# Two colours for tokens in the expert stage of a fused convolution-attention and mixture-of-experts kernel

## The chip, the core and the metric

The kernel runs on one core of one Trainium2 chip. The metric is the device time of one execution in microseconds (us); three runs of the kernel before gave 1347.75, 1349.04 and 1352.04 us, median 1349.04 us. PE is TensorE's matmul, PEld its weight load, DVE is VectorE, ACT ScalarE, POOL GpSimd, SP SyncE.

## What is computed

The input is x, 4 images of 256 channels and 64 x 64 pixels, float32. Layer 0 normalises x, then each pixel attends to its 3 x 3 neighbours, and the result is added to x. Layer 1 takes the 16384 pixels as tokens of width 256: a gated sum over a window of 64 tokens is added, and then a mixture of 8 experts of which each token uses two:

```
logits = tokens @ router_w.T;  rw, re = top_k(softmax(logits), 2)
rw = rw / rw.sum(-1)
out = tokens
for e in range(8):
    h = gelu(tokens @ w1[e] + b1[e])
    y = h @ w2[e] + b2[e]
    out = out + combine[:, e:e + 1] * y        # combine: rw at the two chosen experts, else 0
```

So every token's row of the output is the sum of its own row and of two experts' rows.

## The kernel before

The tokens are worked on in NB = 32 blocks of 512 (NT = 4 tiles of 128). A loop over g (L1064) weaves four generators, each a step at a time: `attend(g)` (the attention), `ranks(g - 2)`, `tail(g - 1)` (window sum, second normalisation, router, the store of the token's own row by L699) and `produce(g + 1)` (projections). A fifth stream, `experts` (L903), is let run by `follow` up to a number of steps that is due at this point of the loop; the knots of that plan follow from `GROUPS`. The framework then fixes the order of instructions on each engine; an engine takes its instructions in that order and waits on semaphores.

Experts work on **slots** of UP = 256 rows of one expert, in two halves of 128 (U = 2). The way there: `tail` ends with `hot` (which expert is a token's first and second choice) and `chosen` (their sum, L737). `ranks` counts on PE, with a triangle of ones and a square of ones (L764, L767), how many tokens before this one chose each expert, adds up the tiles of the block on DVE (`so_far`, L773), and so has the row of each token in its expert's region of `rows_in`, a buffer in HBM (L776 to L782). `give` (L796) scatters 128 tokens with their weights and their row number to these rows by one indirect DMA of GpSimd; a block needs 8. Rows of blocks 0 to 3 go out at once, `paced` behind a recent ACT instruction; those of later blocks are put on the list `waiting`, from which `give_rows` takes two behind every slot's adds (L1022), or all that a fetch needs (L923).

Blocks come in groups (GROUPS, L85: 13 groups of two blocks and 6 of one). When a group's blocks are ranked, L833 to L877 work out on one partition how many slots each expert has full, and write for each slot the expert and the first row to a table. Group k has 2 n 512/256 slots for its n blocks; the first has 7 fewer and the last 14 more, since only full slots are run before the last group. For the last group, `blank` rows are stored behind each expert's rows by SP (L826, eight DMAs of 256 rows), so that part-filled slots read rows of weight zero whose row number lies behind the output. There are 135 slots, 18 of them in the last group.

A slot runs so: SP reads expert and row from the table and fetches the slot's 2 x 128 rows (L926, one of 7 buffers; it waits for the scattered rows of its group); PE transposes them (L950), ACT copies; PE multiplies with w1 (L962), ACT applies gelu (L968); PE multiplies with w2 (L981); DVE adds the bias (L985) and scales by the token's weight (L986), for each half; GpSimd adds each half's 128 rows to the output by an indirect DMA with add (L999). These three PE steps belong to three slots in one round: transposes of slot m + 2, first product of m + 1, second of m.

[...]`add` therefore puts a wait into both adds of a slot, on both adds of the slot before:

```python
behind = adds[-U:]
...
for t in range(U):
    inst = nc.gpsimd.indirect_dma_start(out=out, ..., compute_op=ALU.add).ins
```

Within a slot all tokens are different, so its two halves need not wait for each other.

Of the kernel before, what the change touches and what calls it, by code (L numbers as in the profile page):

```python
# [44 lines left out]
FP = mybir.dt.float32  # L47
AF = mybir.ActivationFunctionType
ALU = mybir.AluOpType
# [3 lines left out]
P = 128  # L53
# [9 lines left out]
def hybrid_block_kernel(ctx: ExitStack, tc: tile.TileContext, ins: dict, out: bass.AP):  # L63
# [20 lines left out]
    ENG = mybir.EngineType  # L84
    GROUPS = (*[2] * 13, *[1] * 6)  # L85
    assert sum(GROUPS) == NB
# [5 lines left out]
    slots_of = [2 * n * TB // UP for n in GROUPS]  # L92
    slots_of[0] -= E - 1
    slots_of[-1] += 2 * (E - 1)
    assert slots_of[0] > 0
    first_slot = [sum(slots_of[:k]) for k in range(len(GROUPS) + 1)]
    SLOTS = max(slots_of)
    N = B * HW
    ROOM = N + UP

# [203 lines left out]
    favour = iota("favour", [P, NT, E], [[0, NT], [-1, E]], base=E)  # L304
    region = iota("region", [P, E], [[ROOM, E]])
    place = iota("place", [P, NT], [[P, NT]], by_partition=1)
# [6 lines left out]
    slot_no = iota("slot_no", [1, SLOTS], [[1, SLOTS]])  # L313
    slot_row = iota("slot_row", [1, SLOTS], [[UP, SLOTS]])

# [11 lines left out]
    )  # L327
    rows_in = hbm.tile([E * ROOM + UP, RW], FP, tag="rows_in", name="rows_in")

    def rows_at(at):  # L330
        return rows_in[bass.ds(at, UP), :].rearrange("(t p) r -> p t r", p=P)

    nc.sync.dma_start(rows_at(E * ROOM), blank)
    stored = [
        nc.sync.dma_start(
            out[N:, :].rearrange("(t p) c -> p t c", p=P), blank[:, :, 0:C]
        ).ins
# [170 lines left out]

    wxs, sums, table, norm1 = {}, {}, {}, {}
    hots, chosens, tokens = {}, {}, {}  # L510
    dispatched = {k: [] for k in range(len(GROUPS))}
# [84 lines left out]
    def tail(g):  # L596
# [39 lines left out]

        wx = w2p.tile([P, NT, C + 1 + E], FP, tag="wx", name=f"wx_{g}")
        wxs[g] = wx
        nc.scalar.activation(z, z, AF.Exp, scale=-1.0)
# [15 lines left out]

        wl = w1p.tile([P, NT, C + 1 + E], FP, tag="wl", name=f"wl_{g}")
        if i == 0:
            nc.vector.memset(wl[WIN:P, 0, :], 0.0)
        else:
            nc.scalar.copy(wl[WIN:P, 0, :], wxs[g - 1][WIN:P, NT - 1, :])  # L660
        nc.scalar.copy(wl[WIN:P, 1:NT, :], wx[WIN:P, 0 : NT - 1, :])
        nc.scalar.copy(wl[0:WIN], wx[0:WIN])
        yield
# [71 lines left out]

        chosen = w2p.tile([P, NT, E], FP, tag="chosen", name=f"chosen_{g}")
        nc.vector.tensor_add(chosen, hot[:, 0], hot[:, 1])  # L737
        weight = w2p.tile([P, 2, NT, E], FP, tag="weight", name=f"weight_{g}")
# [12 lines left out]
    def ranks(g):  # L751
        if not 0 <= g < NB:
# [3 lines left out]
        hot = hots.pop(g)  # L756
        chosen, tok = chosens.pop(g), tokens.pop(g)

        yield
        yield  # L760

        psk = ps_a.tile([P, 2, NT, E], FP, tag="a", name=f"psk2_{g}")
        flat = chosen.rearrange("p t e -> p (t e)")
        nc.tensor.matmul(  # L764
            psk[:, 0].rearrange("p t e -> p (t e)"), before_, flat, start=True, stop=True
        )
        nc.tensor.matmul(  # L767
            psk[:, 1].rearrange("p t e -> p (t e)"), ones, flat, start=True, stop=True
        )
        so_far = w2p.tile([P, NT + 1, E], FP, tag="so_far", name=f"so_far_{g}")  # L770
        nc.vector.tensor_copy(so_far[:, 0, :], region if g == 0 else sums[g - 1][:, NT, :])
        for t in range(NT):
            nc.vector.tensor_add(so_far[:, t + 1, :], so_far[:, t, :], psk[:, 1, t, :])  # L773
        sums[g] = so_far
        row = w2p.tile([P, NT, E], FP, tag="row", name=f"row_{g}")
        nc.vector.tensor_add(row, psk[:, 0], so_far[:, 0:NT, :])  # L776
        own = w2p.tile([P, 2, NT, E], FP, tag="own", name=f"own_{g}")
        nc.vector.tensor_mul(own, hot, row.unsqueeze(1).to_broadcast([P, 2, NT, E]))
        rowf = w2p.tile([P, 2, NT], FP, tag="rowf", name=f"rowf_{g}")
# [22 lines left out]


        for t in range(NT):
            for c in range(2):
                if g < first_of[2]:
                    dispatch(paced(give(t, c)).ins)
                else:
                    waiting.append((k, lambda t=t, c=c: in_turn(
                        dispatch(give(t, c).ins), adds[-1:], given_rows  # L810
                    )))
            yield
# [4 lines left out]
        if final:  # L817

            pad = w2p.tile([1, E], I32, tag="pad", name=f"pad_{k}")
            nc.vector.tensor_copy(pad, so_far[0:1, NT, :])  # L820
            for e in range(E):
                at = nc.values_load(
                    pad[0:1, e : e + 1], engines=[ENG.SP], min_val=0, max_val=E * ROOM - UP,
                    skip_runtime_bounds_check_because=IN_RANGE,
                )
                dispatch(nc.sync.dma_start(rows_at(at), blank).ins)  # L826
            yield

        def small(name, shape=(1, E), dtype=FP):
            return w1p.tile(list(shape), dtype, tag=name, name=f"{name}_{k}")  # L830


        full = small("full", dtype=I32)  # L833
        nc.vector.scalar_tensor_tensor(
            full, so_far[0:1, NT, :], float(UP - 1) if final else 0.0, region[0:1],
            ALU.add, ALU.subtract,
        )
        nc.vector.tensor_single_scalar(full, full, UP.bit_length() - 1, op=ALU.arith_shift_right)
        slots, ends, end, start = small("slots"), small("ends", (1, E, E)), small("end"), small("start")
# [8 lines left out]
        nc.vector.scalar_tensor_tensor(  # L848
            base[:, 0:E], base[:, 0:E], float(UP), region[0:1], ALU.mult, ALU.add
        )  # L850
# [52 lines left out]
    def experts():  # L903
# [87 lines left out]
        def add(m, xs):  # L991
            k, n = of[m]

            behind = adds[-U:]
            if n == 0:
                at = 1 + sum(GROUPS[:k])
                behind = behind + stored[0 if k == 0 else at : at + GROUPS[k]]
            for t in range(U):
                inst = nc.gpsimd.indirect_dma_start(  # L999
                    out=out, out_offset=bass.IndirectOffsetOnAxis(  # L1000
                        ap=xs[:, t, C + E : C + E + 1].bitcast(U32), axis=0
                    ),
                    in_=xs[:, t, 0:C], in_offset=None, compute_op=ALU.add,
                ).ins
                tc.declare_no_dep(
                    inst, group="stores", keep=behind, reason="rows of a later group's blocks"
                )
                tc.declare_no_dep(
                    inst, group="adds", keep=behind, reason="behind the slot before, no other"
                )  # L1010
                for d in behind:
                    tc.add_manual_dep(
                        inst, d.name,
                        mybir.DependencyInfo(
                            mybir.DependencyClass.Sync, mybir.DependencyReason.DATA
                        ),
                        reason="sums of one row",
                    )
                tc.add_to_no_dep_group("adds", inst)
                in_turn(inst, given_rows[-2:], [])  # L1020
                adds.append(inst)
# [107 lines left out]
```

## Time and profile before

| | us |
|---|---|
| median of three runs | 1349.04 |
| the profiled execution | 1382.0 |
| its span | 1380.3 |
| PE busy in the span | 1226.2 (89%) |
| DVE busy | 985.0 (71%) |
| ACT busy | 868.9 (63%) |
| POOL busy | 747.4 (54%) |

How to read the lines: a page of the profile gives, for the whole run, the busy share of each engine in 40 slices (a digit is tenths). A timeline gives for each merged run of instructions its start and length in us from the span's start, engine, line, operation and tiles; in brackets stands the engine's idle time ahead of it and what ended it. [...]One matmul of float32 stands in the records as two passes. 270 adds of line L999 took 1602 ns each on average, 256 scatters of line L797 1055 ns.

### The profile page before, as it was taken

The numbers are of one execution on the slowest core, as the hardware profiler recorded it, in microseconds if no ns is written. First come the engines' busy times: TensorE is split into PE (matmuls) and PEld (weight loads), VectorE is DVE, ScalarE is ACT, GpSimd is POOL, SyncE is SP. The second block draws the span as 40 slices with busy tenths as digits, with TensorE's granted clock in tenths as the row PEclk, the third lists the DMA queues.
The fourth block names the chain that finished last, engine by engine and source line by source line (L and its number), as shares of the span: only waits on it lengthen the run. The fifth ranks groups of instructions, "written<-read, shape, count | busy, mean of one in ns | idle before, by whom it ended". The sixth has DMA issues, their size and how long they took to land. (4 is left out here: it accounts for less than half of the span.)

```text
span 1380.3 us, 23327 instructions
## 1 busy us (share of the span) xinstructions
PE 1226.2 (89%) x6232; PEld 982.6 (71%) x6232; DVE 985.0 (71%) x4653; ACT 868.9 (63%) x1693; POOL 747.4 (54%) x616
## 2 busy tenths in 40 slices
PE   5887999899999999999999999999999998767770
PEld 4666767687878877787878777887878777556550
DVE  4499889688887877787878777877858778522220
ACT  1454577577777776787777776877776676323320
POOL 2023325566665655665666556665655666754444
PEclk8999999999999999999999999999999999989995
DMA  9723355566656665666655565656565546665543
GB/s 316 261 90 131 116 172 123 152 145 146 155 129 157 148 142 144 153 161 151 161 132 140 138 142 106 151 118 146 135 135 118 112 86 145 146 144 83 81 70 38
DMA packets 147794, 190.44 MB, mean 138 GB/s; under 512 B 13776, under 2 KB 121936, under 8 KB 147536
## 3 DMA queue, kind: packets, MB, share of 16 engines
q0 software_dynamic: 51168, 71.07, 29.4%
q1 hardware_dynamic: 94000, 116.42, 27.6%
q10 hardware_dynamic: 2496, 1.45, 0.4%
q8 instruction: 52, 0.85, 0.3%
q14 instruction: 78, 0.64, 0.2%
HBM read 98.31 MB, written 90.59 MB: 137 GB/s over the span
## 5 line engine op out<-in xcount | busy, mean ns | idle before, releaser
L999 POOL DMA_INDIRECT out<-sx x270 | 432.5, 1602 | 427.5 <-DVE sx L986 188.6
L797 POOL DMA_INDIRECT rows_in<-tok,rows x256 | 270.1, 1055 | 124.3 <-issue 65.0
L981 PE MATMUL psy<-w,h 128*128 x1080 | 287.5, 390 | 9.6 <-DVE sx L985 8.4
L962 PE MATMUL psh<-xc,w1s 128*128 128x256 f32 x1080 | 263.9, 387 | 3.9 <-DVE sx L985 3.4
L981 PEld LDWEIGHTS psy<-w,h 128*128 128x128 f32 x1080 | 199.1, 192 | 64.8 <-DVE sx L985 27.6
L962 PEld LDWEIGHTS psh<-xc,w1s 128*128 128x128 f32 x1080 | 203.7, 195 | 32.1 <-DVE sx L985 4.3
L985 DVE TENSOR_TENSOR sx<-psy,b2b 128x256 f32<-128x256 f32 x270 | 113.0, 419 | 141.7 <-PE psy L981 129.3
L968 ACT ACTIVATE h<-psh,w1s 128x256 f32<-128x256 f32 x270 | 113.8, 470 | 98.9 <-PE psh L962 85.4
L460 PE MATMUL psv<-vo,x 128*128 128x257 f32 x528 | 131.1, 391 | 30.9 <-DVE x L442 15.5
L460 PEld LDWEIGHTS psv<-vo,x 128*128 128x128 f32 x528 | 99.0, 195 | 50.5 <-PE psh L962 16.3
L954 ACT COPY xc<-ptx 128x512 f32<-128x512 f32 x135 | 79.0, 585 | 81.3 <-PE ptx L950 62.6
L950 PE MATMUL ptx<-ident,sx 128*128 128x128 f32 x540 | 87.2, 280 | 47.1 <-DMA sx<-rows_in 44.9
L540 PE MATMUL pss<-x,q 128*128 128x256 f32 x512 | 124.3, 385 | 3.6 <-ACT xc L608 3.2
L486 PE MATMUL psq<-x,qk 128*128 128x512 f32 x256 | 123.9, 592 | 0.0
L577 PE MATMUL psc<-v,pT 128*128 128x256 f32 x512 | 121.2, 379 | 0.0
L950 PEld LDWEIGHTS ptx<-ident,sx 128*128 128x128 f32 x540 | 67.5, 147 | 71.5 <-issue 54.5
L577 PEld LDWEIGHTS psc<-v,pT 128*128 128x128 f32 x512 | 96.9, 189 | 26.0 <-issue 13.2
L540 PEld LDWEIGHTS pss<-x,q 128*128 128x128 f32 x512 | 93.0, 190 | 24.4 <-issue 6.9
L986 DVE TENSOR_SCALAR sx<-sx 128x256 f32<-128x256 f32 x270 | 99.9, 370 | 3.1 <-issue 0.2
L968 ACT ACT_TABLE_LOAD x76 | 97.5, 1283 | 0.8
L581 DVE SCALAR_TENSOR_TENSOR xT<-psc,den,xT 128x256 f32<-128x256 f32 x128 | 55.8, 477 | 56.4 <-PE psc L577 53.2
L943 ACT COPY w1s<-w1b 128x514 f32 x135 | 83.7, 620 | 8.6 <-ACT pj L630 4.1
(192 smaller groups left out, 2190.5 us busy)
## 6 DMA issues: line engine op xcount, KB each, us to landing
sx<-rows_in SPq DMA_DIRECT2D x135, 272.0 KB
xs<-in_x SPq DMA_DIRECT2D x32, 512.0 KB
xT<-in_xT SPq DMA_DIRECT2D x32, 512.0 KB
out<-xT SPq DMA_DIRECT2D x32, 512.0 KB
x<-in_x SPq DMA_DIRECT2D x24, 640.0 KB
x<-in_x SPq DMA_DIRECT2D x8, 576.0 KB
out<-sx POOLq DMA_INDIRECT x270
rows_in<-tok,rows POOLq DMA_INDIRECT x256
```

The lines of the kernel that those rows point to most:

```text
L460: nc.tensor.matmul(ps, t[:, ci, j * P : (j + 1) * P], vo[:, ci, :], start=(ci == 0), stop=(ci == NC - 1),)
L486: nc.tensor.matmul(ps, qk[:, ci, co * P : (co + 1) * P], t[:, ci, W : W + TB], start=(ci == 0), stop=(ci == NC - 1),)
L540: nc.tensor.matmul(ps, q[:, ci, t * P : (t + 1) * P], t_[:, ci, t * P : t * P + NK], start=(ci == 0), stop=(ci == NC - 1),)
L577: nc.tensor.matmul(ps[:, u, :], pT[:, u, j, :], vals[j], start=(j == 0), stop=(j == 1))
L797: return nc.gpsimd.indirect_dma_start(out=rows_in[:, :], out_offset=bass.IndirectOffsetOnAxis(ap=rows[:, c, t : t + 1], axis=0), in_=tok[: ...
L950: nc.tensor.transpose(pt[:, c, t * P : (t + 1) * P], xs[:, t, c * P : (c + 1) * P], ident)
L962: nc.tensor.matmul(ps[:, f, :], w1s[:, o : o + P], xc[:, ci, :], start=(ci == 0), stop=(ci == NC - 1),)
L968: inst = nc.scalar.activation(h[:, f, :], ps[:, f, :], AF.Gelu, bias=w1s[:, F1 + f : F1 + f + 1])
L981: nc.tensor.matmul(ps[:, t, :], h[:, f, t * P : (t + 1) * P], w2[:, e, f, :], start=(f == 0), stop=(f == NC - 1),)
L985: nc.vector.tensor_add(ys[:, t, :], ps[:, t, :], b2b[:, e, :])
L986: nc.vector.tensor_scalar_mul(ys[:, t, :], ys[:, t, :], xs[:, t, bass.ds(e + C, 1)])
L999: inst = nc.gpsimd.indirect_dma_start(out=out, out_offset=bass.IndirectOffsetOnAxis(ap=xs[:, t, C + E : C + E + 1].bitcast(U32), axis=0), ...
```

## The change

Each token gets one of two colours, 0 or 1. Tokens that chose the same pair of experts take them in turn. A region of `rows_in` exists for each expert and colour (16 for 8), and a slot is 128 rows of colour 0 and 128 rows of colour 1 of one expert. Both rows of a token have its colour, so the first half of a slot can only meet rows of first halves, and the second of second halves. An add waits only for the add of the same half of the slot before.

To find the colours, `tail` works out for the 28 pairs of experts which pair each token has (`both`) and the running sum over the block's four tiles (`upto_t`). `ranks` multiplies these on PE with the triangle, and a history of earlier blocks (`earlier`) with the square of ones, into one PSUM tile; DVE adds 2^23, so that the count's lowest bit is the float's lowest bit, masks by the token's own pair, reduces, and takes the bit. From there `hot` is split by colour, and the ranks are counted over 16 columns for 8.

Besides: the number of full slots of an expert is the smaller of its two colours' (the larger in the last group); the first group has three blocks and there are 11 of two and 7 of one; the first group has 8 slots fewer and the last 16 more (136 slots in all, 20 in the last group). Rows of blocks 0 to 6 and of the last two go out at once instead of behind adds. The padding is 136 rows for each of 16 regions, written from 68 partitions, from `blank` for colour 0 and `zeros` for colour 1. `wl`, the left neighbour of the window sum, is one constant tile with a fifth column that keeps the last tile of the block before, so that `wx` needs one buffer.

```diff
-    GROUPS = (*[2] * 13, *[1] * 6)
+    GROUPS = (3, *[2] * 11, *[1] * 7)
...
-    slots_of[0] -= E - 1
-    slots_of[-1] += 2 * (E - 1)
+    slots_of[0] -= E
+    slots_of[-1] += 2 * E
...
-    ROOM = N + UP
+    PAD = P + E
+    ROOM = N // 2 + 2 * P
+    HALF = E * ROOM + P
...
     def rows_at(at):
-        return rows_in[bass.ds(at, UP), :].rearrange("(t p) r -> p t r", p=P)
+        return rows_in.rearrange("(t n) r -> n t r", t=U)[bass.ds(at, P)]
...
-        wx = w2p.tile([P, NT, C + 1 + E], FP, tag="wx", name=f"wx_{g}")
-        wxs[g] = wx
+        wx = w1p.tile([P, NT, C + 1 + E], FP, tag="wx", name=f"wx_{g}")
...
-        wl = w1p.tile([P, NT, C + 1 + E], FP, tag="wl", name=f"wl_{g}")
         if i == 0:
             nc.vector.memset(wl[WIN:P, 0, :], 0.0)
         else:
-            nc.scalar.copy(wl[WIN:P, 0, :], wxs[g - 1][WIN:P, NT - 1, :])
-        nc.scalar.copy(wl[WIN:P, 1:NT, :], wx[WIN:P, 0 : NT - 1, :])
-        nc.scalar.copy(wl[0:WIN], wx[0:WIN])
+            nc.scalar.copy(wl[WIN:P, 0, :], wl[WIN:P, NT, :])
+        nc.scalar.copy(wl[WIN:P, 1:, :], wx[WIN:P])
+        nc.scalar.copy(wl[0:WIN, 0:NT, :], wx[0:WIN])
...
-        chosen = w2p.tile([P, NT, E], FP, tag="chosen", name=f"chosen_{g}")
-        nc.vector.tensor_add(chosen, hot[:, 0], hot[:, 1])
+        chosen = w2p.tile([P, NT, 2, E], FP, tag="chosen", name=f"chosen_{g}")
+        nc.vector.tensor_add(
+            chosen, *(hot[:, c].unsqueeze(2).to_broadcast([P, NT, 2, E]) for c in range(2))
+        )
+        both = w2p.tile([P, NT, PAIRS], FP, tag="both", name=f"both_{g}")
...
+        nc.vector.tensor_mul(
+            both[:, :, 0 : D * E].rearrange("p t (d e) -> p t d e", e=E),
+            at.unsqueeze(2).to_broadcast([P, NT, D, E]), ahead,
+        )
+        nc.vector.tensor_mul(both[:, :, D * E :], at[:, :, 0:H], at[:, :, H:])
+        upto_t = w2p.tile([P, NT, PAIRS], FP, tag="upto_t", name=f"upto_t_{g}")
+        nc.vector.tensor_copy(upto_t[:, 0, :], both[:, 0, :])
+        for t in range(1, NT):
+            nc.vector.tensor_add(upto_t[:, t, :], upto_t[:, t - 1, :], both[:, t, :])
...
+        psr = ps_a.tile([P, PAIRS], FP, tag="a", name=f"psk0_{g}")
+        nc.tensor.matmul(psr, ones, earlier, start=True, stop=False)
+        nc.tensor.matmul(psr, before_, upto_t[:, NT - 1, :], start=False, stop=True)
+        yield
+        nc.vector.tensor_add(earlier, earlier, upto_t[:, NT - 1, :])
...
+        nc.vector.scalar_tensor_tensor(
+            seen, upto_t, float(2**23), psr.unsqueeze(1).to_broadcast([P, NT, PAIRS]),
+            ALU.add, ALU.add,
+        )
+        nc.vector.tensor_mul(seen, seen, both)
...
+        nc.vector.tensor_reduce(odd, seen, AX.X, ALU.add)
...
+        nc.vector.tensor_single_scalar(colour[:, :, 1], odd.bitcast(I32), 1, op=ALU.bitwise_and)
+        nc.vector.tensor_scalar(colour[:, :, 0], colour[:, :, 1], -1.0, 1.0, ALU.mult, ALU.add)
...
+        for c in range(2):
+            nc.vector.tensor_mul(
+                each[:, c], hot[:, c].unsqueeze(2).to_broadcast([P, NT, U, E]),
+                colour.unsqueeze(3).to_broadcast([P, NT, U, E]),
+            )
...
+        nc.vector.tensor_add(
+            by_colour, *(each[:, c].rearrange("p t k e -> p t (k e)") for c in range(2))
+        )
+        yield
+        psk = ps_a.tile([P, 2, NT, U * E], FP, tag="a", name=f"psk2_{g}")
+        flat = by_colour.rearrange("p t e -> p (t e)")
...
         for t in range(NT):
             for c in range(2):
-                if g < first_of[2]:
+                if not first_of[3] <= g < NB - 2:
+                    give_rows(0, k)
                     dispatch(paced(give(t, c)).ins)
...
-            for e in range(E):
+            H = PAD // U
+            for e in range(U * E):
                 at = nc.values_load(
...
-                dispatch(nc.sync.dma_start(rows_at(at), blank).ins)
+                dispatch(nc.sync.dma_start(
+                    rows_in[bass.ds(at, PAD), :].rearrange("(t p) r -> p t r", p=H),
+                    (blank, zeros[:, :, 0:RW])[e // E][0:H],
+                ).ins)
...
+        nc.vector.tensor_tensor(
+            full, count[:, 0], count[:, 1], ALU.max if final else ALU.min
+        )
-        nc.vector.tensor_single_scalar(full, full, UP.bit_length() - 1, op=ALU.arith_shift_right)
+        nc.vector.tensor_single_scalar(full, full, P.bit_length() - 1, op=ALU.arith_shift_right)
...
-            behind = adds[-U:]
-            if n == 0:
-                at = 1 + sum(GROUPS[:k])
-                behind = behind + stored[0 if k == 0 else at : at + GROUPS[k]]
+            at = 1 + sum(GROUPS[:k])
+            first = stored[0 if k == 0 else at : at + GROUPS[k]] if n == 0 else []
             for t in range(U):
+                behind = adds[-U:][:1] + first
```

## The prediction

> **What bounds the kernel now.** I read the page first, then busy time by stretch, the timelines of single engines, and the order in which each engine holds the instructions of the two versions. The page's row of slices divides the run into three stages:
>
> ```profile
> PE   5887999899999999999999999999999998767770
> DVE  4499889688887877787878777877858778522220
> ```
>
> One slice is 34.5 us. TensorE is full from the sixth slice to the thirty-third, and thin in the last six, where DVE is nearly idle. Busy time by stretch (columns: stretch, length, then PE, PEld, DVE, ACT, POOL busy, granted clock, DMA share, GB/s):
>
> ```profile
> 99.00:122.00 23.00, 19.20 (x103) 14.47 (x103) 21.49 (x121) 12.09 (x30) 8.44 (x9) 1.00 0.35 118
> 600.00:700.00 100.00, 98.53 (x511) 79.14 (x510) 82.38 (x381) 75.87 (x141) 62.30 (x47) 1.00 0.63 144
> 1267.00:1310.00 43.00, 31.41 (x139) 25.67 (x140) 10.60 (x28) 13.46 (x27) 20.11 (x13) 0.92 0.54 82
> ```
>
> Early (about 75 to 205 us, before experts run) DVE is busy 21.5 of 23 us: DVE-bound. In the middle PE is busy 98.5 of 100 at full clock and its matmuls start 216 ns apart, one behind the other; DVE has 18% left. At the end nothing is full, so a wait decides. The GpSimd timeline there:
>
> ```profile
> 1271.78 1.55 POOL L999 DMA_INDIRECT out<-sx  x1 [3.11 <-DMA out<-sx]
> 1273.63 1.55 POOL L999 DMA_INDIRECT out<-sx  x1 [0.30 <-issue]
> 1278.18 1.55 POOL L999 DMA_INDIRECT out<-sx  x1 [3.00 <-DMA out<-sx]
> 1280.03 1.55 POOL L999 DMA_INDIRECT out<-sx  x1 [0.31 <-issue]
> ```
>
> Each pair is one slot's two adds. The second starts 1.85 us after the first; the next slot's first waits for the second's landing, 4.55 to 4.75 us after that one's start (here 1273.63 to 1278.18). So a slot takes about 6.5 us, and from 1232.40 to 1369.67 there are 22 slots at 137.27/21 = 6.54 us. TensorE could go faster; its timeline in the same stage, before the fetched rows run out of buffers:
>
> ```profile
> 1235.29 0.60 PE L950 MATMUL ptx<-ident,sx 128*128 128x128 f32 x4
> 1239.53 0.60 PE L950 MATMUL ptx<-ident,sx 128*128 128x128 f32 x4
> 1243.76 0.60 PE L950 MATMUL ptx<-ident,sx 128*128 128x128 f32 x4
> ```
>
> Slots are 4.24 us apart. The chain of waits ends in the same add, wait, add sequence. When does that stage begin? SP's timeline:
>
> ```profile
> 1201.23 0.42 SPq L699 DMA_DIRECT2D out<-xT  x1
> 1202.16 3.44 SPq L826 DMA_DIRECT2D rows_in<-blank  x3
> 1208.78 0.40 SPq L926 DMA_DIRECT2D sx<-rows_in  x1
> 1209.72 5.63 SPq L826 DMA_DIRECT2D rows_in<-blank  x5
> 1225.89 6.26 SPq L926 DMA_DIRECT2D sx<-rows_in  x3
> ```
>
> The last group's first fetch leaves at 1225.89 (call it T0), when the last of block 31's scattered rows has landed (the chain has that transfer from 1222.95 to 1225.40). The padding DMAs were done before it.
>
> **The last stage.** An add now waits for the same half of the slot before. That is start to start 4.65 us (the middle of the 4.55 to 4.76 seen) for each half; GpSimd itself needs 2 x 1.85 = 3.70 and PE 4.24, so the period falls from 6.5 to 4.65. The last group has 20 slots for 18 (and the kernel 136 for 135 in all). Before: T0 to the end 1380.3 - 1225.9 = 154.4 us. After: the first slot of the group reaches its add after 3.2 us of fetch, three rounds of PE (3 x 4.24) and 0.8 us of DVE, about 17 us; then 19 x 4.65 = 88.4; then 10.6 from the last pair to the end (1369.67 to 1380.3). Sum 116, so -38.4 us.
>
> **Where that stage begins.** The last two blocks' rows go out as soon as they are ranked, not two behind every slot's adds. Block 31's ranks are ready at 1189.22, and its rows left from 1197.27 to 1223.93, spread over four slots; eight in one go take 8 x 1.28 = 10 us. Block 30's, ranked at 1163, left until 1193; PE waits for them up to 1198.6. Both waits go. What is late next is SP: 16 padding DMAs in place of 8, in one go, ahead of the group's first fetch. In the rows shown five of them start (5.63 - 0.38)/4 = 1.3 us apart, so 16 take 21 us. Here a rule of the Trainium skill speaks against the change: "DMA: Bandwidth & Descriptors", the section on why a DMA increments its semaphore by 16, says that a DMA's share of the engines is the largest number up to 16 that divides the outer dimension. The old padding has 128 partitions (16 engines); the new has 68, so 4. The trace's 1088-byte packets of the padding take 48 ns each; 136 of them on 4 engines are 34 x 48 = 1.63 us, and 16 DMAs on the same 4 engines 26 us. No transfer of this trace has a partition count other than 128, so the rule is not shown; by the row 21 us, by the rule 26 (an estimate from both). I take 26. Padding can begin when the counts are there, 1190 plus about 4 us of the new ranking, instead of 1202: 1194 + 26 + 3 to land = 1223, so T0 moves -3 us (by the row -8; a worst case, were the fetch in front of the padding held by an add as at 1208.78, +6).
>
> **What DVE gets.** The order of instructions has 16 more small DVE instructions per block (507 for 32 blocks): pair products 2, running sums 4, the history 1, seen/odd/colour 5, halves 3, the other widths one net. The nearest rows: 158 ns for 8 wide (L773), 181 for 32 (L737), 212 for 64 (L778), so about 1 ns an element and 260 for the 112 wide ones: 3.2 us a block as durations. But such instructions overlap: their starts are 102 ns apart at the median, both early and in the middle. By starts it is about 2.2 us a block. Early, DVE-bound, five blocks pay it: 11 us, of which DVE's remaining 7% takes some; I take 9 (ends 0 and 16). In the middle, DVE goes from 82 to about 88 of 100: hidden under PE, as long as no PE instruction waits for it.
>
> **What PE gets.** Two more matmuls a block. The nearest row is the old pair:
>
> ```profile
> 482.19 0.31 PE L764 MATMUL psk<-chosen,before 128*128 128x32 f32 x2
> 482.33 0.39 PE L767 MATMUL psk<-chosen,ones 128*128 128x32 f32 x2
> 482.56 0.63 PE L950 MATMUL ptx<-ident,sx 128*128 128x128 f32 x4
> ```
>
> Each takes two passes about 0.11 us apart, as a 128 wide transpose's do, so width 64 in place of 32 costs nothing and the two new ones 0.44 us. PE is full for about 26 blocks: +11.4. One slot fewer lies ahead of the last group (116 for 117): -4.2.
>
> **The new wait.** The rank matmuls now wait for DVE's colours, which wait for a PE product of the same block. Behind them on PE stand psq of the next block and the slot's psy; behind psq ACT's q, behind psy DVE's own bias add. In the new order some 6 us of matmuls stand between the product and the ranks, and ten DVE instructions (about 2 to 3 us with the slot work between). One more PSUM tile per block turns through the same five buffers. Ends: 0 and 1.5 us a block; PE's excess over packed matmuls is already about 1.5 us a block there, mostly for DVE, and DVE gets 7% fuller; I take 0.3, so 26 x 0.3 = +8.
>
> **Costed at nothing.** ACT copies 265 more columns a block (1.07 for 0.85 us), behind 25% idle ACT; uncovered, 7 us. The single wx buffer waits for matmuls a block older. Giving the first seven blocks' rows directly rather than four finds GpSimd under half busy. The larger first group only shifts slots.
>
> **The sum.** Early +9, PE +11.4 - 4.2, wait +8: +24. T0 -3, last stage -38.4. Against the profiled execution, -17 on 1382.0, or 1365. That execution is 33 us above the median of the runs, and the trace doesn't say where; the packed matmuls can't stretch, the indirect transfers may. With half of it in the last 26 slots a slot there was 5.9 us before, and the new period is PE's 4.24: the stage then gives 154.4 - 22 x 0.63 = 140.5 against 17 + 19 x 4.24 + 10 = 107.6, -33. So -33 - 3 + 24 = -12: 1337 us.
>
> **The rivals.**
> *The middle becomes a PE-DVE ping-pong (slower).* Place: PE at the rank matmuls, waiting for the colours. For it: DVE at 88% and in strict order, with two 0.4 us slot operations per half among the ten. Against: the 6 us of cover. It decides from 0.3 + 12/26 = 0.76 us a block; at 1.5 us it costs 31 more: 1368. Chance 0.24.
> *The halves don't overlap.* If the transfers queue behind one another, the period stays at 6.5: the stage is 17 + 19 x 6.5 + 10.6 = 151, and only the costs stay: about 1366. Against it: the two halves' packets are seen 1.85 us apart, each over in 1.6 us. Chance 0.05.
> *The gain is the profile's.* If all 33 us lie in the last 26 slots, a slot was 5.2 us, the stage 126.5, and -19 - 3 + 24 = +2: 1351. Chance 0.13.
> *The new DVE work is hidden throughout.* Costs shrink to about 7, and T0 comes 8 earlier: 1349 - 33 - 8 + 7 = 1315. Chance 0.14.
> *The forecast,* 1337, with its own range 1325 to 1345: 0.44.
>
> A measurement tells about 0.3%, 4 us, from no change. Faster by more: 0.44 + 0.14 = 0.58; within: 0.13; slower: 0.29. The range reaches from 1315 to the slower cases: 1314 to 1366.
>
> **What would show it.** After: pairs of adds 4.2 to 4.7 us apart in the last twenty slots; the padding's landing as the release of the group's first fetch, and whether 16 of them take 21 or 26 us; block 10's begin some 10 us later than before, and each block of the middle 0.4 to 0.8 us longer, with no wait of the rank matmuls for DVE over 0.5 us. Wrong would make me: adds still 6.5 us apart, or middle blocks over 1.2 us longer.

## The result and the profile after

The changed kernel takes 1384.80 us (median of 4 runs, 1381.80 to 1385.39) against 1349.86 us of the kernel before in the same session: 1.0254 of it, 95% interval 1.0231 to 1.0277. It is slower by 2.5%, where 1337 us, faster, was forecast, and it lies above the range.

The kernel before takes 1347.5 to 1350 us in three of the five sessions below and 1380 to 1384 us in the other two, each session on another chip, and the profile of before in the prediction (1382.0 us) is of the longer kind; so times are compared as ratios within one session. The run **e0** (before, unchanged: 1348.27 us, ratio 1.000 [0.9991, 1.0009], span 1346.8) gives the profile of before to set beside that of the changed kernel (span 1379.3).

> The kernel before, unchanged. The profiled execution of before took 1382.0 us against 1349.9 us in its runs, while that of the changed kernel took 1381.8 against 1384.8. If the profile adds time of itself, wherever adds are chained, the profiled execution here is again some 30 us above the runs. If that one execution was merely a slow one, the profile here shows a span near 1350, and its timeline shows where the 30 us had been.

The profile adds no such time: e0's profiled execution took 1348.48 us, as its runs did. The slices of the changed kernel:

```profile
PE   5988797999999999999999999999999999844982
DVE  4488989898888887888979897888778889721331
```

PE is full from the eighth slice on, for the sixth in the row of before, and the thin end is now broken in two: a hollow (8, 4, 4), then nearly full (9, 8). Busy time by stretch in the changed kernel (length, PE, PEld, DVE, ACT, POOL, granted clock, DMA share, GB/s):

```profile
600.00:700.00 100.00, 99.75 (x517) 79.55 (x517) 84.31 (x400) 78.57 (x148) 60.72 (x47) 1.00 0.65 155
1200.00:1267.00 67.00, 28.76 (x122) 23.87 (x123) 13.05 (x55) 10.65 (x22) 32.11 (x25) 0.69 0.57 128
1267.00:1310.00 43.00, 40.19 (x205) 34.34 (x203) 17.34 (x42) 21.06 (x43) 26.11 (x17) 1.00 0.69 108
```

and of e0 in the middle:

```profile
600.00:700.00 100.00, 100.00 (x534) 81.79 (x533) 83.88 (x399) 78.32 (x151) 62.37 (x49) 1.00 0.61 146
```

Between 1200 and 1267 PE works 43% of the time. After 1267 it works 93%, where before it was 73% in this stretch: the relaxed adds do what was forecast, after a hole that wasn't. In the middle PE looks equally busy in both, but 517 matmuls lie in the 100 us for 534, and a block takes 38.0 us for 37.1 (mean from block 10 to block 31): here a busy share near 100% hides short gaps.

Where the 32.5 us between the two profiled spans lie, beside what the prediction's terms give for each stretch. The marks are the add of the output bias to x in blocks 10 and 31 (`xT<-xT,outb`; blocks count from 0), the cast of block 31's row numbers, the last group's first fetch (T0) and the end:

| us | before (e0) | after | difference | forecast |
|---|---|---|---|---|
| start to block 10 | 304.6 | 322.6 | +18.0 | +9 |
| block 10 to block 31 | 778.1 | 798.6 | +20.5 | +15 |
| from there to the rows of block 31 | 74.7 | 86.5 | +11.8 | +4 |
| from there to T0 | 36.1 | 47.8 | +11.7 | -7 |
| T0 to the end | 153.3 | 123.9 | -29.4 | -38 |

(The forecast for the middle is 11.4 - 4.2 + 8; the -3 for T0 holds the 4 us of longer ranking, which have their own row here.) Ahead of T0 every stretch came out worse than forecast, 50.3 us up to the rows of block 31 alone; only the last stage went the way that was forecast, by 9 us less. GpSimd's timeline in the last group of the changed kernel:

```profile
1315.47 1.55 POOL L1082 DMA_INDIRECT out<-sx  x1 [2.06 <-DVE sx L1070]
1317.32 1.55 POOL L1082 DMA_INDIRECT out<-sx  x1 [0.30 <-issue]
1320.23 1.55 POOL L1082 DMA_INDIRECT out<-sx  x1 [1.36 <-issue]
1322.08 1.55 POOL L1082 DMA_INDIRECT out<-sx  x1 [0.30 <-issue]
```

These pairs are 4.76 us apart (4.87 in the mean of the last 18 slots) and wait for DVE's scaled rows or for nothing that the profile shows; the 3 us for a landing between pairs are gone.

### The profile page after: what moved, and what is told of

It is laid out like the page before. It is cut to its first block, busy times and chain, and to the rows that moved or that the text cites. A ratio compares the mean times of both kernels' runs of the same rounds, so it can differ in the third digit from the quotient of the medians.

```text
span 1379.3 us, 24259 instructions
## 1 busy us (share of the span) xinstructions
PE 1248.3 (91%) x6380; PEld 999.0 (72%) x6380; DVE 1051.8 (76%) x5159; ACT 878.4 (64%) x1699; POOL 750.7 (54%) x619
## 5 line engine op out<-in xcount | busy, mean ns | idle before, releaser
L1082 POOL DMA_INDIRECT out<-sx x272 | 451.4, 1660 | 388.6 <-DVE sx L1070 103.8
L869 POOL DMA_INDIRECT rows_in<-tok,rows x256 | 254.4, 994 | 160.0 <-issue 81.7
L1046 PE MATMUL psh<-xc,w1s 128*128 128x256 f32 x1088 | 267.6, 384 | 0.0
L1046 PEld LDWEIGHTS psh<-xc,w1s 128*128 128x128 f32 x1088 | 199.9, 192 | 23.2 <-issue 0.5
L1038 ACT COPY xc<-ptx 128x512 f32<-128x512 f32 x136 | 80.0, 588 | 81.3 <-PE ptx L1034 81.1
L624 ACT COPY xc<-ptx 128x512 f32<-128x512 f32 x64 | 34.3, 589 | 123.8 <-PE ptx L621 123.8
```

The lines of the kernel that those rows point to most:

```text
L869: return nc.gpsimd.indirect_dma_start(out=rows_in[:, :], out_offset=bass.IndirectOffsetOnAxis(ap=rows[:, c, t : t + 1], axis=0), in_=tok[: ...
L1046: nc.tensor.matmul(ps[:, f, :], w1s[:, o : o + P], xc[:, ci, :], start=(ci == 0), stop=(ci == NC - 1),)
L1082: inst = nc.gpsimd.indirect_dma_start(out=out, out_offset=bass.IndirectOffsetOnAxis(ap=xs[:, t, C + E : C + E + 1].bitcast(U32), axis=0), ...
```

## The last stage: e1, e2, e3, e7

SP's timeline of the changed kernel around T0:

```profile
1214.28 0.37 SPq L1010 DMA_DIRECT2D sx<-rows_in  x1
1215.27 13.46 SPq L902 DMA_DIRECT2D rows_in<-blank  x8
1229.66 16.56 SPq L902 DMA_DIRECT2D rows_in<-zeros  x8
1255.46 86.45 SPq L1010 DMA_DIRECT2D sx<-rows_in  x20
```

The 16 padding DMAs (L902) hold SP for 31 us, and T0 is 9 us behind the last of them. What they need was there with block 31's ranks, at 1207.7. But the fetch ahead of them on SP comes, in the chain of waits, after two adds' transfers,

```profile
1206.80 7.28 DMA out<-sx x2
1214.28 0.37 SPq L1010
```

so the padding queued behind a fetch that waited for adds, the case that the prediction priced at +6 and set aside.

**e1**: the padding is 160 rows from 80 partitions; more bytes, but a partition count that 16 divides.

```diff
-    PAD = P + E
+    PAD = P + 4 * E
```

> The changed kernel with 160 instead of 136 padding rows a region, so 80 instead of 68 partitions, which 16 divides. Theory: the 16 padding transfers run on 4 DMA engines and hold the last group's first fetch for 40 us (1215.3 to 1255.5); on 16 engines they take 21 to 24 us at the issue rate of before, and the kernel gets 13 to 18 us faster (1384.8 to about 1369). Rival: SP's own loading of 16 row numbers and its eight semaphores set the 40 us; then it is the same, or 3 us slower for the 18% more bytes.

Measured: 1.0083 [1.0058, 1.0108], 23 us below the changed kernel's 2.54%; the profiled span is 25.5 us shorter (1353.8). SP's timeline:

```profile
1213.90 8.49 SPq L902 DMA_DIRECT2D rows_in<-blank  x8
1223.03 8.62 SPq L902 DMA_DIRECT2D rows_in<-zeros  x8
1234.61 83.69 SPq L1010 DMA_DIRECT2D sx<-rows_in  x20
```

18 us for 31, and T0 follows 3 us behind, not 9: 21 us of the gain are here. The packets in the traces fit the reason: counted by their starts and lengths, 3.3 packets of the padding are in flight at a time in the changed kernel (1218.5 to 1252 us) and 8.3 in e1 (1217 to 1234 us). Block 31's rows are cast at 1206.3, as late as in the changed kernel (1207.7), so the padding has no part in the 50 us. A repetition in the session of e9 to e11 (**e8**) gave 1.0094 [1.0063, 1.0125].

> The kernel of e1 once more, beside the next ones, so that they are compared on one chip: 0.8% slower than before, as there.

**e2, e3**: eight empty slots more in the last group, in the kernel before and in the changed one (`slots_of[-1]` + 8). They read padding and add zero rows behind the output.

> The kernel before with 8 more slots in its last group, which read empty rows and add zeros behind the output: the price of one slot of the last stage, measured in runs without a profile. If the profile shows this stage as it is, 8 x 6.5 = 52 us more. If the profile stretches it, 8 x 5.0 = 40 us or less.

> The same 8 slots more in the changed kernel. By the step of the prediction, a slot of the last stage costs 4.65 us: 37 us more; by its profile some 4.9: 39. If the halves don't help in runs without a profile, as much as in the kernel before.

Measured: e2 1.0350 [1.0326, 1.0374], 1395.55 us: 47.5 us over the session's 1348.07, so 5.94 us a slot. e3 1.0535 [1.0500, 1.0570], 1421.2 us: 36.4 over the changed kernel's 1384.8 (from another session), so 4.55 us a slot. The prediction had 5.9 and 4.24 in runs (6.5 and 4.65 in the profile). That 5.9 is met is luck: in the profiles of e0 and e2, at the level of the runs, the last 18 slots' adds start 6.50 us apart, as in the profile of before (6.53). e2's added slots come out cheaper because its run ends 5.3 us after its last add begins, e0's 8.9. In the changed kernel adds are 4.87 us apart, in e3 5.06 and in e1 4.57: near the 4.65 of the profile's terms, and not PE's 4.24.

**e7**: e1 with the wait of before, each add on both halves of the slot before; all else as e1.

```diff
-                behind = adds[-U:][:1] + first
+                behind = adds[-U - t :][:U] + first
```

> The changed kernel with the 160 row padding, but each add waits for both halves of the slot before, as in the kernel before. The difference to e1 is what the relaxed wait gives. From the slots measured one by one (5.94 for 4.55 us): 20 x 1.39 = 28 us slower than e1, 1386. Rival: TensorE and the fetches bound the last stage, and the wait gives under 10.

Measured: 1.0417 [1.0350, 1.0484], against e1's 1.0083 and e8's 1.0094: the one line is worth 3.2 to 3.3% of before, 45 us, more than expected. e8 is the same kernel as e1 in a session of the longer kind, as e7's is, so their profiles can be compared. T0 to the end takes 167.9 us in e7, with 6.54 us a slot, and 125.6 in e8, with 4.87: 42 us, of which the period is 19 x 1.67 = 32. T0 itself is 12 us later in e7 (1275.8 for 1263.4), for which the prediction had no term. The rival that the halves don't overlap is out. (The code gives this wait's reason as `sums of one row`. No run here leaves the wait out, so what the output would lose without it isn't shown.)

## What the colours cost: e4, e5, e6, e9, e10, e11

**e4**: the kernel before with all of the colours' work; the two colours are summed again ahead of the ranks (`chosen` = colour 0 + colour 1), so that rows, slots and adds stay those of before. **e5**: only its DVE instructions, which nothing reads. **e6**: only its two matmuls, on a tile of zeros, unread. In outline, with the tails of e4 and e5 left out:

```diff
         yield
+        psr = ps_a.tile([P, PAIRS], FP, tag="a", name=f"psk0_{g}")
+        nc.tensor.matmul(psr, ones, earlier, start=True, stop=False)
+        nc.tensor.matmul(psr, before_, upto_t[:, NT - 1, :], start=False, stop=True)
+        yield
+        nc.vector.tensor_add(earlier, earlier, upto_t[:, NT - 1, :])
...
         yield
```

> The kernel before with the colours worked out in every block (pairs, running sums, history, two matmuls, colours, halves of hot) and then summed again to what it had, so that slots, adds, padding and groups stay. It has the new DVE work, the new matmuls and the wait of the rank matmuls for the colours, and nothing of the gain. Theory: this work is what makes block 31's ranks 50 us late (1207.7 for 1157.4 in an undisturbed profile of before): 35 to 45 us slower than before. Rival: the groups of three and one and the rows that go out directly cost most of it; then this is 10 to 20 us slower.

> Only the DVE part of e4: 16 to 17 more small DVE instructions a block that nobody waits for, no matmuls. If DVE's own fullness is the cost (early, where it bounds, and in the middle through late normalised rows), 20 to 30 us slower; if the cost is PE's matmuls and the wait, some 9 us (early blocks alone).

> Only the two matmuls a block of 28 columns on constant data, which nobody reads. By the step of the prediction 26 x 0.44 = 11 us slower.

Measured: e4 1.0306 [1.0261, 1.0352]; e5 1.0208 [1.0175, 1.0241]; e6 0.9998 [0.9987, 1.0010]. The two matmuls on a full PE, forecast at 11 us, cost nothing. In e6's profile PE is busy 791 of the 800 us from 300 to 1100, in that of before 779, with the same span of 1380.3: the new matmuls filled PE's short gaps. The unread DVE work, with the step that comes with it (below), costs 2.1%, 28 us, three times the term for DVE. What e4 has beyond e5, the chain from PE to DVE and back, the matmuls and one more add, costs a further 1.0%; with the matmuls at nothing (e6) the chain is the likely part, but no run shows it alone.

**e9**: before with the changed kernel's groups only (`GROUPS = (3, *[2] * 11, *[1] * 7)`). **e10**: the changed kernel, but a token's colour is read from its place: tiles 0 and 3 of a block are colour 0, tiles 1 and 2 colour 1, so no pairs are counted, and the padding is 256 rows. **e11**: e10 with the groups of before, the last rows going out behind adds again, and 135 slots. In e10 and e11 the two halves of an expert are no longer kept within a known difference of each other (with these inputs it reaches 103 rows); for inputs that lean more the padding would not do.

```diff
-        both, upto_t = pairs_of.pop(g)
...
+        for to, of, by in ((2, 1, 1), (3, 0, 0), (4, 3, 3), (5, 2, 2)):
+            nc.vector.tensor_add(so_far[:, to, :], so_far[:, of, :], psk[:, 1, by, :])
```

> The kernel before with only the groups of the changed one (three blocks, eleven times two, seven times one). Theory: the groups only shift slots, within 5 us of before. Rival: the later start of the experts leaves TensorE empty early and costs the 16 us that the changed kernel has lost by its ninth block.

> The changed kernel with colours that need no work: tokens of tiles 0 and 3 of a block have colour 0, those of tiles 1 and 2 colour 1. Slots, relaxed waits, groups and direct rows stay; the padding is 256 rows, since the halves of an expert then differ by up to 103 rows with these inputs (no bound holds for others). If the colours' work costs what e4 showed, 3%, this is 2 to 2.5% faster than before, about 30 us; if the loss came from groups, direct rows or padding, it stays near e8.

> As e10, but with the groups of before and the rows of the last blocks behind the adds as before, so: the kernel before with halves by tile, relaxed waits and 16 paddings. If groups and direct rows help, 5 to 15 us slower than e10; if they cost, as much faster.

Measured: e9 0.9955 [0.9935, 0.9975]; the groups are no cost. e10 0.9710 [0.9694, 0.9727], e11 0.9672 [0.9656, 0.9689]: with the colours for nothing, the relaxed adds make the kernel 2.9 and 3.3% faster than before. e10 minus e11, 6 us, is groups, direct rows and one slot together. e8 minus e10, on one chip, is what the colours themselves cost, with their step and their wait: 1395.5 - 1344.6 = 51 us (padding from 80 partitions in e8, from 128 in e10). Nearly all of it, 47 us, lies ahead of T0 (1263.4 for 1216.2).

These pieces account for the result: colours 51, narrow padding 23, relaxed adds -45, groups with direct rows and the slot 6: +35 us, as measured. They come from different sessions and each is known to a few us, so that the sum is met so closely is luck.

## Why the colours cost that: e12, e13, e15, e16, e17

After e5 my theory was the amount of DVE work in the early stage. **e12** and **e13** are e5 with the unread DVE work only in blocks 8 to 31 (the condition below, around both of its parts), and only in blocks 0 to 7 (`g < 8`):

```diff
+        if g >= 8:
```

> The kernel before with the colours' DVE work, unread, only in blocks 8 to 31 (24 of 32). Theory: DVE has room there and PE waits for none of it: at most 0.5% slower, the ratio 1.000 to 1.005, block 9 begins within 3 us of before. Rival (the work costs where PE is full, at each block alike): 24/32 of the 2.1% of the run with all blocks, 1.6% slower.

> The kernel before with the colours' DVE work, unread, only in blocks 0 to 7. Theory: DVE is full there, so 16 instructions a block cost their 3.2 to 3.8 us and nothing wins it back: 1.4 to 2.0% slower (20 to 27 us), block 9 begins some 20 us late and block 31 as late as that. Rival (cost at each block alike): 8/32 of 2.1%, 0.5% slower. A second rival: the work is lost early but won back in the middle, where slots are drawn in as there is room: under 0.5%.

Measured: e12 1.0223 [1.0203, 1.0242], e13 1.0218 [1.0193, 1.0243]. Each alone costs what all of it costs in e5 (1.0208). So it isn't the work, early or late: theory and rival both fell. What all three share, and e6, e9, e10 and e11 lack, is one more step in `ranks`: the generator stops once more in each turn of the loop, so a turn has 28 or 31 steps for 27 or 30. **e15** is the kernel before with that step alone. No work is added: both profiles have 6232 records of PE and 4653 of DVE.

```diff
         yield
         yield
+        yield
 
         psk = ps_a.tile([P, 2, NT, E], FP, tag="a", name=f"psk2_{g}")
```

> The kernel before with one bare step (yield) more in ranks and nothing else: no instruction is added, only the order in which slots' work is woven between the blocks' changes. Theory (the step is what cost in the runs with the colours' DVE work): 1.5 to 2.2% slower. Rival (the DVE work costs, by something that does not grow with its amount, its tiles for instance): within 0.3% of before.

Measured: 1.0195 [1.0176, 1.0213], 26 us. The intervals of e5, e12 and e13 overlap with it: on top of the step, 16 DVE instructions a block cost about 0.1 to 0.3%, which the intervals hardly tell from nothing.

How does an empty step cost 26 us? It puts the products of the ranks later on PE: behind block products (psp, psv, psc) in place of ahead of them. DVE's order changes with it. Two places of the early stage in e0 (the last line is the normalised x of the next block):

```profile
142.82 0.16 DVE L773 TENSOR_TENSOR so_far<-so_far,psk 128x8 f32<-128x8 f32 x1 [0.93 <-PE psk L767]
144.20 0.35 DVE L625 SCALAR_TENSOR_TENSOR pj<-psp,trstd_a,bp 128x128 f32<-128x128 f32 x1 [0.82 <-PE psp L619]
...
187.17 0.56 DVE L442 TENSOR_SCALAR x<-x,imean,irc 128x576 f32<-128x576 f32 x1
```

and in e15:

```profile
144.71 0.61 DVE L625 SCALAR_TENSOR_TENSOR pj<-psp,trstd_a,bp 128x128 f32<-128x128 f32 x2 [3.93 <-PE psp L619]
...
193.49 1.04 DVE L442 TENSOR_SCALAR x<-x,imean,irc 128x576 f32<-128x576 f32 x2
194.09 3.80 PE L460 MATMUL psv<-vo,x 128*128 128x257 f32 x8 [7.00 <-DVE x L442]
```

At the first place psk comes later, so DVE stands for 3.93 us at psp's reader; the block as such loses little there (the add of the output bias starts at 150.91 for 150.54). The second place costs more. In e15 the end of `ranks`, which works out the slots of a group (L833 to L877 of before), falls on DVE between 184.5 and 192.1 us, right ahead of x; in e0 it was over by 182.6. DVE is busy 10.00 of the 10 us from 185 to 195, x comes at 193.49, and PE waits 7.00 us for it. PE is slow behind that wait too: these eight records of psv take 3.80 us, the next eight, at 199.72, 1.90; the granted clock is 0.50 from 194 to 198 us, and 0.90 from 150 to 200, where e0 has 1.00. Block 6 is 3 us late, block 8 9.5.

The waits between 95 and 300 us (us in total, times, longest), e0:

```profile
PE psv L460 <- DVE x L442: 6.9, 3, 3.7
...
DVE xT L581 <- PE psc L577: 4.0, 3, 1.6
...
DVE pj L625 <- PE psp L619: 2.0, 5, 0.8
```

and e15:

```profile
PE psv L460 <- DVE x L442: 18.4, 5, 7.5
...
DVE xT L581 <- PE psc L577: 12.5, 10, 5.1
DVE pj L625 <- PE psp L619: 10.2, 4, 3.9
```

PE waits for the normalised x of the next block (L442), DVE for PE's products: the two hold each other up in turn, and each is less busy for it. Between 150 and 200 us PE is busy 40.0 us in e15 and 45.5 in e0, DVE 43.2 and 46.2. e15 has lost 9.5 us at block 9, 12 at block 10 and 22 at block 31; in the middle it loses half a microsecond a block. The step also counts in the plan that lets slots run (`follow`), and e15 doesn't part the two.

How much an order costs may itself depend on small shifts of time. The kernel before, unchanged, loses 10 us against e0 by block 10 in its profile of the longer kind (314.5 for 304.6), with one wait of DVE of 7.4 us that e0 doesn't have.

The changed kernel in the same stretch, 95 to 300 us:

```profile
PE ptx L1034 <- DMA sx<-rows_in: 6.6, 1, 6.6
PE psv L471 <- DVE x L453: 5.7, 3, 2.7
PE psk L836 <- DVE by_colour L828: 5.0, 3, 2.4
PE psp L635 <- DVE stop L561: 4.2, 1, 4.2
```

PE and DVE wait on each other here too, but at other pairs; the rank products' wait for colours is one of four. So it is shown on the kernel before that the step costs, and read from its trace how; in the changed kernel the same is seen only in a mixed form. Can the changed kernel be rid of it? **e16** is e1 with the colours' product moved ahead of ranks' first step, so that a turn has as many steps as before. **e17** is e1 with its step, and the plan scaled to it.

```diff
-        yield
-
         both, upto_t = pairs_of.pop(g)
```

```diff
-    STEPS, LAG = {NB: 14, NB + 1: 8}, 0.35
+    STEPS, LAG = {NB: 15, NB + 1: 9}, 0.35
...
-                follow(g + min(n / STEPS.get(g, 26), 0.999))
+                follow(g + min(n / STEPS.get(g, 27), 0.999))
```

> The changed kernel with the padding of 160 rows (ratios 1.008 and 1.009 of before) and the product for the colours moved ahead of ranks' first step, so that ranks has as many steps as before. All of the colours' work stays. Theory of the step: 1.5 to 2.2% less, 0.987 to 0.994 of before, and so faster than before with the colours as the change has them. Rival (DVE work, or the chain product, colours, ranks): 1.005 to 1.012.

> The changed kernel with the padding of 160 rows and its extra step, but the plan divides by 27 for 26 (15 and 9 in the last two turns for 14 and 8). If the step costs because the plan's due number of slots is reached one step too early in each turn: as the run without the step, 0.987 to 0.994. If it costs because ranks is shifted against the other generators: 1.005 to 1.012.

Measured: e16 1.0312 [1.0276, 1.0347], e17 1.0159 [1.0112, 1.0206], against e1's 1.0083 and e8's 1.0094. e16 is clearly worse and e17 no better: neither the number of steps nor the plan's scale is the cause as such, and both expectations of a gain fell. What e15, e16 and e17 show together is that the order in which the engines hold their instructions is worth about 2%, and that a step put in at one place is not undone by taking one out at another. How much of the changed kernel's 51 us is order, and how much the longer chain to the ranks, stays open; on the kernel before the step was worth 26, and what e4 has beyond e5 13.

**e14**, a try for more: e11 with the eight paddings of colour 1 issued from ACT's queue.

```diff
-                    pad[0:1, e : e + 1], engines=[ENG.SP], min_val=0, max_val=U * HALF - PAD,
+                    pad[0:1, e : e + 1], engines=[(ENG.SP, ENG.Activation)[e // E]], min_val=0, max_val=U * HALF - PAD,
...
-                dispatch(nc.sync.dma_start(
+                dispatch((nc.sync, nc.scalar)[e // E].dma_start(
```

> The kernel with colours by tile and the groups of before (ratio 0.967), with the eight paddings of colour 1 issued from ACT's queue beside SP's eight. SP's row of them took 9.1 us ahead of the last group's first fetch (1206.99 to 1216.1), so theory: that fetch leaves 6 to 9 us earlier and the kernel gains as much, ratio 0.961 to 0.963. Rival: the last scattered rows or the transfers themselves end last there, and the fetch moves by less than 3 us: 0.965 to 0.968.

Measured: 0.9666 [0.9639, 0.9693], the same as e11's 0.9672. ACT's timeline shows what took the place of SP's 9 us (the first line is five of the eight paddings):

```profile
1172.73 12.37 ACTq L848 DMA_DIRECT2D rows_in<-zeros  x5
1185.15 0.84 ACT L998 ACTIVATE h<-psh,w1s 128x256 f32<-128x256 f32 x2 [12.49 <-DMA rows_in<-zeros]
```

The gelu of a slot stood 12.5 us behind padding on ACT, and T0 came 31.8 us after block 31's ranks for 33.6 in e11. A queue's wait was moved to an engine that slots need.

## Why the prediction was wrong

**The step that failed** is the price of the colours. The prediction summed it from durations, +9 for DVE, +11.4 for PE and +8 for the wait, and put the changed order of the engines' instructions at nothing. Measured, the colours cost 51 us where these terms give 28 (e8 less e10), and not by these terms: put alone into the kernel before, the matmuls cost 0, the DVE instructions 0.1 to 0.3% and the extra step, which the sum left out, 26 us. How the 51 us divide inside the changed kernel stays open. The second term that failed is T0: -3 was forecast, and the padding from 68 partitions alone costs 23 us (after less e1).

**The adds' period (-33 in runs, -38 in the profile): the mechanism right, the size in part luck.** 4.87 us a slot where 4.24 to 4.65 was worked out, from the 1.85 us between the halves and the landing; T0 to the end fell by 29.4 us, and by 34.1 in e1. The -33 rests on slots of 5.9 us before, which were 6.5, and of 4.24 after. e7 prices the line at 45 us.

**T0 (-3 after the start of the padding's move): wrong, +12 behind the ranks.** Two terms. The start: the worst case (a fetch held by an add in front of the padding) is what happened. The transfers: the prediction weighed the row, 21 us, against the rule of the Trainium skill ("DMA: Bandwidth & Descriptors", the section on why a DMA increments its semaphore by 16: the share of the engines is the largest divisor of the outer dimension up to 16) and took the rule's 26. The traces agree with the rule: with 80 partitions for 68 the same DMAs issue in 18 us for 31, with 8.3 packets in flight for 3.3. No view names the engines of one DMA, so that they are 4 is not shown as such. And 26 + 3 was still too small: from 1215.27 to T0 it took 40.2 us. The packets took 55 ns in the mean where the sum had 48, and with 3.3 in flight for 4 the 16 x 136 of them take 36 us. The end of the chain there:

```profile
1237.60 6.44 DMA rows_in<-zeros
1244.33 10.86 DMA out<-sx x3
1255.46 3.50 DMA sx<-rows_in
```

SP loads a row number (L898) between any two of the DMAs, and a DMA stands up to 3.6 us at issue (at 1231.07). The chain names three adds' transfers as the last thing ahead of T0, but packets of the padding run until 1253.0 too; which of them held the fetch isn't shown.

**PE, two matmuls a block (+11.4): wrong, 0.** e6 measured them at 0.9998. The step assumed that a full PE has no place for 0.44 us; PE's short gaps took them (busy 791 for 779 of 800 us).

**DVE early (+9): the sign and place right, size and cause wrong.** 18 us were lost by block 10. But the amount of DVE work, which the step counted by starts (16 of them 102 ns apart are 1.6 us a block, where it took 2.2), costs next to nothing on the kernel before (e12, e13 against e15). The prediction took "DVE is full" as the price of more work; what e15 shows in its place is a price of the order in which DVE holds its work.

**The new wait (+8, 0.3 us a block at the rank products): wrong place.** Over the whole run PE waits 5.3 us, in four waits, for the colours. A middle block takes 1.0 us longer, for 0.4 to 0.8, but not there. The rival of the ping-pong (1368 us, 0.24) was right that PE and DVE would wait on each other, and wrong on where: not at the rank products in the middle, at 0.76 us a block or more. In the changed kernel such waits are seen before block 10, at psv and psp as much as at psk; what the middle's 20.5 us are made of isn't shown.

**Costed at nothing, or not at all: the extra step.** `ranks` stops three times ahead of its rank products where it stopped twice, and each stop of a generator is a place in the weave of the loop. It was never costed. On the kernel before it is worth 26 us, more than the whole sum of costs, 24. But e16, without it, is no faster: in the changed kernel its share can't be told from that of the longer chain.

**The 33 us between the shown profile and the median: put in the wrong place.** Half of it was laid in the last 26 slots, since packed matmuls "can't stretch". Beside e0 nearly all of it lies ahead of block 31's ranks (1189.2 there, 1157.4 in e0), where PE is packed; from T0 to the end the two profiles have 154.4 and 153.3. The rival that the gain is only the profile's is out with it.

**Groups, direct rows, the wider ranks:** the groups cost nothing (e9); the others weren't tried alone, and groups, direct rows and the slot more cost 6 us together (e10 less e11).

## What to carry to other kernels

In a kernel whose engines' orders are woven by hand, price a change in the weave first: put the empty step in alone, and see what it costs before the work is added to it. Relaxing a wait that bounds a stage paid; get what it needs from something that is there already (here the tile's place) where that is sound, and not from a new chain across engines. For small DMAs, try a partition count that 16 divides, even at more bytes: here 80 for 68 took 21 us off the last group's first fetch.

## What the hardware showed that was not expected

- 16 DMAs of 136 rows from 68 partitions held SP for 31 us, 16 of 160 rows from 80 partitions for 18 us, with 3.3 and 8.3 of their packets in flight at a time.
- Two more small matmuls per block on a PE that the profile of before shows 98.5 us busy in 100: 0.9998 [0.9987, 1.0010].
- The same work in another order: 1.0195 [1.0176, 1.0213].
- Behind a wait of 7.0 us PE was granted a clock of 0.50 for 4 us, and the same eight records of psv took 3.80 us for 1.90 (e15).
- DMAs issued from ACT's queue held ACT itself for 12.5 us.
